# Second MLP layer of a fused attention block: two of seven products on a second level in six of eight units, with one row operation and one weight fold moved

## The chip, the cores and the metric

The kernel runs on one core of one Trainium2 chip. A core has five engines with queues of their own: TensorE (PE in the profile; its weight loads are the row PEld), VectorE (DVE), ScalarE (ACT), GpSimd (POOL) and SyncE (SP, which here issues DMAs). [...] The metric is the time of one execution on the device in microseconds (us), and the median over runs is compared.

## The reference

Two layers follow one another on an image `x` of 2 x 512 x 32 x 32 values (2 images, 512 channels, 1024 positions), all in float32.

```python
# layer 0: deformable attention with a bias from a small network per pair of positions, then an MLP
xn = bn(x); q = gconv1x1(xn); offsets = tanh(...)*4; kv = grid_sample(xn); k, v = gconv1x1(kv)
bias = relu(relu(pos @ w1) @ w2) @ w3            # for 1024 x 64 pairs, 8 heads, 2 images
x = x + out_w @ softmax(q k^T * scale + bias) v + out_b
xn2 = bn(x)
h1 = gelu(mlp_w1 @ xn2 + mlp_b1)                 # 512 -> 2048 channels
x = x + mlp_w2 @ h1 + mlp_b2                     # 2048 -> 512 channels
# layer 1: full attention over 1024 positions
q, k, v = x Wq^T + bq, x Wk^T + bk, x Wv^T + bv
x = x + (softmax(q k^T / sqrt(512)) v) Wp^T + bp
```

The change is in the MLP of layer 0, and touches two small preparations of layer 1 that run beside it.

## The kernel before

**Three stages.** The bias network takes about the first three quarters of the time (line 695 and its surroundings). Then, from about 1900 us on, come the output projection, the MLP and the attention of layer 1. The MLP lies between 1935 and 2307 us of the profiled span.

**Products.** All large products of the later stages are split once into two by two blocks and done with seven products of blocks instead of eight (the scheme of Strassen in Winograd's form). `PARTS` names, for each product 1 to 7, which of seven weight blocks meets which of seven moving blocks; blocks 4 to 6, and a rewritten block 3 or 1, are sums of the four original ones. `fold` makes the sums of weights, `spread` those of the moving side (four operations on VectorE: lines 125 and 128). A product of blocks is 256 x 256 weights times 256 x 512 values; `multiply` runs it with four matmuls of 512 columns into a pair of PSUM banks and then calls an eviction from `took`. Each float32 matmul is two instructions (passes) in the trace, so a product is 8 passes.

**A second level.** `twice` runs a pair of such products once more split, each into seven products of 128 x 128 weights and 256 columns. One step does one of the seven for both products of the pair: two matmuls of 256 columns, four passes (line 160). Steps share two half banks: steps 1, 6, 7 and 4 accumulate one after the other in one, steps 5 and 3 in another, step 2 has its own. So each result must be taken out before the next step may add to the same half bank. ScalarE (lines 166, 170, 172, 176) and VectorE (`plus`, line 137) take them out.

**The MLP's units.** Eight units (`units`): image b (0, 1) times a quarter p (0 to 3) of the 2048 hidden channels; unit i = 4 b + p. A unit runs `layer1` (512 -> 512 hidden channels, six products in three pairs with `twice`, one plain, then GELU by line 1101, result in the tile `hm`, then `spread` of `hm`) and `layer2` (512 hidden -> 512 channels, seven plain products, line 1082). Of `layer2`'s products four are kept over the units of an image in `acc` (`own`; ScalarE copies in the first unit of an image, line 1157, VectorE adds in the others), three are added into the image `xs` at once (`give`). `finish(b)` combines `acc` and adds the bias `mlp_b2` at the end of an image.

**Weights.** `load_first` and `load_inner` bring the next unit's first-layer weights (tiles `w1x` and `w1t` in turn, inner sums `w1e`), the sums made by accumulating DMAs that POOL issues (line 984, called gathers here). `load_second` loads `w2t` on SP when the unit before has read its last, and POOL folds it with four operations (line 119), behind the last gather in its queue. The point between two units, where `layer2` of one ends and `layer1` of the next begins, is called the seam here.

**Work beside it.** In each unit one row operation (line 1223) multiplies a row block `wr` of layer 1's weights with a bias row `br` and sums it into `ub`; `wr` has the buffer tag "ss" and is loaded by SP (line 1211). `load_g` brings `gg`, a product of layer 1's weights made earlier, with four loads on SP, and POOL folds it. `blocks(0)` makes sums of the finished image 0 with four VectorE operations (lines 971 to 974).

**What sets the order.** The order on each engine is fixed when the kernel is built: a scheduler places instructions by priority in program order, and `tc.issue_after(...)` holds an instruction behind a named one. Pools with a number of buffers decide which tile waits for which. `mq` hands out four PSUM tiles of two banks in turn.

Of the kernel before, what the change touches and what calls it, by code (L numbers as in the profile page):

```python
# [8 lines left out]
F32 = mybir.dt.float32  # L9
# [48 lines left out]
def conv_seq_kernel(ctx: ExitStack, tc: tile.TileContext, x, xt, kst, pst, cst, vec, wsm, outw, w1, w2, wl, wlt, brow, out):  # L58
# [82 lines left out]
    def twice(pool, sets, weights, moving, dest, done, fills=(), sign=-1.0):  # L141
# [3 lines left out]
        for _, g, q in sorted(todo, key=lambda e: e[0]):  # L145
# [31 lines left out]
            elif q == 3:  # L177
                plus(d12, d12, bank)
                done(g)

    FIRST_W, FIRST_X = (1, 0, 2, 3, 4, 5, 6), (1, 4, 0, 6, 5, 2, 3)
    AT_W, AT_X = ((0, 0), (1, 0), (1, 1), (0, 1)), ((0, 0), (0, 1), (1, 0), (1, 1))
# [794 lines left out]
    with ExitStack() as top, tc.tile_pool(name="wp", bufs=1) as wp:  # L977
# [28 lines left out]
        def load_second(i):  # L1006
            if i >= len(units):
                return
            w = wp.tile([P, 7, 2, 256], F32, tag="w2t", name="w2t")
            nc.sync.dma_start(out=w[:, 0:4], in_=w2[:, units[i][1]])  # L1010
            fold(nc.gpsimd, [w[:, j] for j in range(7)])
            wts[units[i]].append(w)

# [137 lines left out]

        def layer2(b, p, w, hm):

# [6 lines left out]
            def give(o2, h, op):  # L1160
                x_ = xs[:, 2 * o2 : 2 * o2 + 2, b, h * 512 : (h + 1) * 512]
                return lambda ps: plus(x_, x_, ps, op)

            multiply(mq, (2, 1, 3, 5, 6, 7, 4), product(w, hm), {
                1: own(0), 5: own(1), 6: own(2), 7: own(3),
                2: give(0, 0, ALU.add), 3: give(0, 1, ALU.add), 4: give(1, 0, ALU.subtract),
            })

        def finish(b):
            p1, p5, p6, p7 = (acc[:, j] for j in range(4))  # L1170
            for o in range(NCH):
# [32 lines left out]
        for i, (b, p) in enumerate(units):  # L1204
# [7 lines left out]
            with tc.issue_after(copied[-1]) if i else nullcontext():  # L1212
                load_first(i + 1)
            wa, we, wb = wts.pop((b, p))
            hm = cp.tile([P, 7, 2, 512], F32, tag="big", name="hm")
            layer1(p, we, wa, xb, xe, hm, ((4, lambda: part(1)), (10, lambda: part(2))) if p == 0 else (), i == 0)
            if i == NU:
# [3 lines left out]

            with tc.issue_after(newest(mybir.EngineType.DVE)):
                nc.vector.scalar_tensor_tensor(
                    wr, wr, 1.0, br, ALU.mult, ALU.mult, accum_out=ub[:, j, k : k + 1]
                )
            if p == NU - 1 and b == 0:
                xb = normalise(1)
            layer2(b, p, wb, hm)
            load_second(i + 1)
            if i == NU:  # L1230
                with tc.issue_after(newest(mybir.EngineType.SP)):
                    gg = f_pool.tile([P, 7, 2, 256], F32, tag="vp", name="gg")
                    load_g(gg, 0)
            if i == NU + 2:
                xbl = blocks(0)
# [368 lines left out]
```

## Time and profile before

| | us |
|---|---|
| median of 3 runs (2612.23 to 2612.84) | 2612.61 |
| the profiled execution | 2612.25 |
| its span | 2610.5 |
| MLP in the span, 1935.3 to 2307.2 | 371.9 |
| TensorE busy in it | 369.7 |
| VectorE busy in it | 255.6 |
| ScalarE busy in it | 120.8 |
| POOL busy in it | 117.9 |

The granted TensorE clock is 1.00 throughout the MLP, and the 16 DMA engines are busy for 0.66 of it. The busy times come from the view of windows. A line of the timeline has start, duration, engine, source line, operation, output<-input, shape and count, and in brackets how long the engine stood idle before and what released it. Consecutive like operations of an engine are merged into one line, so a duration can cover several. Matmuls overlap one another, and a matmul line's duration reaches past the start of the next one: the rate is read from starts.

### The profile page before, as it was taken

The numbers are of one execution on the slowest core, as the hardware profiler recorded it, in microseconds if no ns is written. First come the engines' busy times: TensorE is split into PE (matmuls) and PEld (weight loads), VectorE is DVE, ScalarE is ACT, GpSimd is POOL, SyncE is SP. The second block draws the span as 40 slices with busy tenths as digits, with TensorE's granted clock in tenths as the row PEclk, the third lists the DMA queues.
The fourth block names the chain that finished last, engine by engine and source line by source line (L and its number), as shares of the span: only waits on it lengthen the run. The fifth ranks groups of instructions, "written<-read, shape, count | busy, mean of one in ns | idle before, by whom it ended". The sixth has DMA issues, their size and how long they took to land.

```text
span 2610.5 us, 49004 instructions
## 1 busy us (share of the span) xinstructions
PE 2597.5 (100%) x19660; PEld 1009.8 (39%) x19660; DVE 2303.7 (88%) x1459; ACT 1754.3 (67%) x2362; POOL 980.6 (38%) x1122
## 2 busy tenths in 40 slices
PE   9999999999999999999999999999999999999999
PEld 3332333333233233223333333332355655646656
DVE  6999999999999999999999999999776587666656
ACT  5887888888888888888788777777733242314041
POOL 1344444444444444444454444333322334200100
PEclk9999999999999999999999999999999999999999
DMA  5889999999998999899999899888777768400202
GB/s 187 173 192 197 194 194 195 195 189 191 200 191 189 188 204 203 175 191 202 191 197 192 186 193 193 176 174 186 153 200 171 147 148 167 91 16 1 73 1 56
DMA packets 177634, 428.27 MB, mean 164 GB/s; under 512 B 30048, under 2 KB 78320, under 8 KB 174720
## 3 DMA queue, kind: packets, MB, share of 16 engines
q0 software_dynamic: 107392, 273.09, 58.4%
q1 hardware_dynamic: 69584, 151.75, 17.5%
q8 instruction: 155, 2.54, 0.4%
q14 instruction: 71, 0.58, 0.1%
q10 hardware_dynamic: 432, 0.31, 0.0%
HBM read 82.16 MB, written 6.55 MB: 34 GB/s over the span
## 4 chain that ended last, share of the span: by engine, by line
PE 96%; DVE 3%; ACT 1%; issue 0%; DMA 0%; DVEq 0%; ACTq 0%
PE ps L695 67%; PE sw L1082 7%; PE sw L1253 7%; PE sw L160 7%; PE sw L1029 2%; PE sw L1351 2%; PE psg L597 1%; PE sim L828 1%; DVE hm L137 1%; PE psx L1329 1%; PE sim L809 0%; PE pt L845 0%; PE pkv L534 0%; PE pb L880 0%; PE psq L333 0%
## 5 line engine op out<-in xcount | busy, mean ns | idle before, releaser
L695 PE MATMUL ps<-h,cw 128*32 128x512 f32 x16384 | 1772.0, 592 | 1.8 <-ACT rx L708 1.0
L678 DVE CUSTOM_DVE_ANT_1 h<-ta,tb 128x4096 f32<-128x4096 f32 (+1 forms) x257 | 1131.3, 4402 | 28.9 <-PE ps L695 24.0
L695 PEld LDWEIGHTS ps<-h,cw 128*32 128x32 f32 x16384 | 527.7, 110 | 1214.0 <-issue 1160.4
L708 ACT ACTIVATE rx<-ps,sc 128x1024 f32<-128x1024 f32 x512 | 568.6, 1111 | 138.4 <-PE ps L695 115.5
L737 POOL DMA_DIRECT2D u<-u x394 | 406.9, 1514 | 2.5 <-issue 2.2
L710 ACT ACTIVATE ub<-ps,sc 128x1024 f32<-128x1024 f32 x256 | 308.4, 1205 | 90.6 <-PE ps L695 90.5
L720 POOL DMA_DIRECT2D uo<-ub x127 | 111.4, 877 | 600.1 <-DVE ub L718 570.0
L718 DVE SCALAR_TENSOR_TENSOR ub<-rx,sc,ub 128x1024 f32<-128x1024 f32 x256 | 327.3, 1278 | 3.1 <-ACT ub L710 3.1
L1082 PE MATMUL sw<-hm,w2t 128*128 128x512 f32 x448 | 194.0, 592 | 0.2 <-DVE hm L125 0.2
L710 ACT ACTIVATE uo<-ps,sc 128x1024 f32<-128x1024 f32 x128 | 154.3, 1205 | 43.9 <-PE ps L695 40.7
L718 DVE SCALAR_TENSOR_TENSOR uo<-rx,sc,uo 128x1024 f32<-128x1024 f32 x128 | 163.7, 1279 | 7.6 <-ACT uo L710 7.0
L737 POOL DMA_DIRECT2D u<-uc x124 | 124.8, 1280 | 17.6 <-DMA u<-uc 15.3
L1082 PEld LDWEIGHTS sw<-hm,w2t 128*128 128x128 f32 x448 | 84.9, 190 | 104.0 <-issue 97.9
L720 POOL DMA_DIRECT2D uc<-ub x64 | 55.4, 866 | 179.9 <-DVE ub L718 147.9
L137 DVE TENSOR_TENSOR hm<-hm,sw 128x512 f32<-128x512 f32 x79 | 57.6, 732 | 73.0 <-PE sw L160 50.6
L720 POOL DMA_DIRECT2D u<-ub x62 | 53.1, 856 | 178.8 <-DVE ub L718 178.8
L737 POOL DMA_DIRECT2D uc<-uc x63 | 107.6, 1708 | 0.0
L737 POOL DMA_DIRECT2D uc<-uo x63 | 102.8, 1632 | 10.6 <-DMA uc<-uo 10.3
L1417 POOL DMA_DIRECT2D xs<-rs x6 | 7.2, 1200 | 259.6 <-DVE rs L137 259.6
L737 POOL DMA_DIRECT2D u<-uo x62 | 84.8, 1368 | 21.6 <-DMA u<-uo 18.4
L658 ACT ACTIVATE ta<-fb,vs 128x512 f32<-128x512 f32 (+1 forms) x65 | 89.1, 1374 | 5.6 <-DMA fb<-fdr 5.6
L710 ACT ACTIVATE uc<-ps,sc 128x1024 f32<-128x1024 f32 x64 | 77.0, 1203 | 21.2 <-PE ps L695 19.3
(306 smaller groups left out, 2648.2 us busy)
## 6 DMA issues: line engine op xcount, KB each, us to landing
uo<-ub POOLq DMA_DIRECT2D x127, 512.0 KB, 5.4
fb<-fdr SPq DMA_DIRECT2D x64, 512.0 KB, 5.7
uc<-ub POOLq DMA_DIRECT2D x64, 512.0 KB, 6.0
u<-ub POOLq DMA_DIRECT2D x62, 512.0 KB, 6.3
uc<-uc POOLq DMA_DIRECT2D x63, 256.0 KB, 8.3
uc<-uo SPq DMA_DIRECT2D x63, 256.0 KB, 3.2
uc<-uo POOLq DMA_DIRECT2D x63, 256.0 KB, 5.7
u<-u POOLq DMA_DIRECT2D x62, 256.0 KB, 6.9
```

The costliest lines, as they stand in the source:

```text
L137: nc.vector.tensor_tensor(out, a, b_, op)
L160: nc.tensor.matmul(bank[:, e, :], w, x, start=(q in (1, 2, 5) and e == k == 0), stop=True, skip_group_check=True,)
L658: nc.scalar.activation(ta.rearrange("p j x -> p x j")[:, :, j0:j1], fb[:, 0, :, j0:j1], AF.Identity, bias=col("cb1"), scale=col("w1x"),)
L678: nc.vector._custom_dve(TENSOR_ADD_SAT, out=h1[:, y : y + step].rearrange("p y t x -> p (y t x)"), in0=a.unsqueeze(1).to_broadcast([P, ste ...
L695: nc.tensor.matmul(ps[32 * q : 32 * q + 32, h, :], cw2[:, 32 * z : 32 * z + 32], h1[:, 16 * h : 16 * h + 16, q, :], start=True, stop=True,)
L708: nc.scalar.activation(o, ps, AF.Relu, bias=sc[:, 4 + z : 5 + z])
L710: nc.scalar.activation(o, ps, AF.Relu, bias=sc[:, 4 + z : 5 + z], scale=sc[:, z : z + 1])
L718: nc.vector.scalar_tensor_tensor(r[1], r[0], sc[:, z : z + 1], r[1], ALU.mult, ALU.add)
L720: nc.gpsimd.dma_start(out=sums[s][1], in_=sums[s][3], accum_op=ALU.add)
L737: nc.gpsimd.dma_start(out=out, in_=in_, accum_op=ALU.add)
L1082: nc.tensor.matmul(ps[:, m, :], w[:, a, k, m * P : (m + 1) * P], x[:, b_, k, :], start=(k == 0), stop=(k == 1),)
L1253: nc.tensor.matmul(ps[:, m, :], w[:, a, k, c + m * P : c + (m + 1) * P], x[b_][:, k, :], start=(k == 0), stop=(k == nk - 1),)
```

## The change

In units 0, 1, 2, 5, 6 and 7 `layer2` runs products 7 and 6 on the second level. They form one pair: steps 2 and 1 come after four plain products (2, 1, 3, 5), then product 4, then steps 6, 5, 7, 3, 4. Units 3 and 4 keep seven plain products in the old order. The pair's moving side needs three inner sums from `spread(xi)`, four VectorE operations of 128 x 512 values; two go into a new eighth block of `hm`, one into `hme`, a tile with the tag "ss" that `wr` also uses. Its weights need three inner sums in the new tile `w2e` and one rewritten block, four POOL operations behind each fold of `w2t`. `acc` blocks 2 and 3 swap the products that they keep.

The row operation moves from between `layer1` and `layer2` into `layer1`, at place 15.5 among its steps (after step 2 of the third pair, before step 4 of the second). `load_g` of `gg` moves from the end of unit 4 to ahead of `layer2` of unit 5.

```diff
@@ -178,6 +178,7 @@
                 plus(d12, d12, bank)
                 done(g)
 
+    TWO = slice(3, 6, 2)
     FIRST_W, FIRST_X = (1, 0, 2, 3, 4, 5, 6), (1, 4, 0, 6, 5, 2, 3)
     AT_W, AT_X = ((0, 0), (1, 0), (1, 1), (0, 1)), ((0, 0), (0, 1), (1, 0), (1, 1))
 
@@ -1009,7 +1010,11 @@
             w = wp.tile([P, 7, 2, 256], F32, tag="w2t", name="w2t")
             nc.sync.dma_start(out=w[:, 0:4], in_=w2[:, units[i][1]])
             fold(nc.gpsimd, [w[:, j] for j in range(7)])
-            wts[units[i]].append(w)
+            we = None
+            if i not in (NU - 1, NU):
+                we = wp.tile([P, 2, 3, P], F32, name="w2e")
+                fold(nc.gpsimd, inner_w(w, we, TWO, slice(0, 2)))
+            wts[units[i]] += [w, we]
 
         for i, (b, h) in enumerate(halves):
             for o in range(NCH):
@@ -1149,7 +1154,7 @@
             twice(mq, ((1, 6), (4, 7), (5, 3)), weights, moving, dest, done, (*plain, *others))
             spread([hm[:, j] for j in range(7)])
 
-        def layer2(b, p, w, hm):
+        def layer2(b, p, w, hm, we=None):
 
             def own(j):
                 a = acc[:, j]
@@ -1161,13 +1166,66 @@
                 x_ = xs[:, 2 * o2 : 2 * o2 + 2, b, h * 512 : (h + 1) * 512]
                 return lambda ps: plus(x_, x_, ps, op)
 
-            multiply(mq, (2, 1, 3, 5, 6, 7, 4), product(w, hm), {
-                1: own(0), 5: own(1), 6: own(2), 7: own(3),
+            took = {
+                1: own(0), 5: own(1), 7: own(2), 6: own(3),
                 2: give(0, 0, ALU.add), 3: give(0, 1, ALU.add), 4: give(1, 0, ALU.subtract),
-            })
+            }
+            plain = product(w, hm)
+            if we is None:
+                multiply(mq, (2, 1, 3, 5, 6, 7, 4), plain, took)
+                return
+
+            far = hm[:, 7].rearrange("p a (b n) -> p a b n", n=256)
+            last = f_pool.tile([P, 2, 256], F32, tag="ss", name="hme")
+            xi = [hm[:, 1:6:4, k, 256 * n : 256 * n + 256] for k, n in AT_X] + [far[:, 0], far[:, 1], last]
+            wi = inner_w(w, we, TWO, slice(0, 2))
+            d11, d12, d21, d22 = (acc[:, 2:4, m, 256 * h : 256 * h + 256] for m in range(2) for h in range(2))
+
+            def into(d, bank, op=ALU.add, new=False):
+                if new and p == 0:
+                    nc.scalar.activation(d, bank, AF.Copy, scale=1.0 if op == ALU.add else -1.0)
+                else:
+                    plus(d, d, bank, op)
+
+            def inner(bank, q):
+                u, t = PARTS[q]
+                with tc.issue_after(newest(mybir.EngineType.PE)):
+                    for e in range(2):
+                        nc.tensor.matmul(
+                            bank[:, e, :], wi[u][:, e], xi[t][:, e], start=(q in (1, 2, 5) and e == 0), stop=True,
+                            skip_group_check=True,
+                        )
+
+            def whole(q):
+                with tc.issue_after(newest(mybir.EngineType.PE)):
+                    multiply(mq, (q,), plain, took)
+
+            for q in (2, 1, 3):
+                whole(q)
+            with tc.issue_after(newest(mybir.EngineType.DVE)):
+                spread(xi)
+            whole(5)
+            side, main = (mq.tile([P, 2, 512], F32, tag="ps2", name="sw") for _ in range(2))
+            two, five = (side[:, h].rearrange("p (e n) -> p e n", e=2) for h in range(2))
+            one = main[:, 0].rearrange("p (e n) -> p e n", e=2)
+            inner(two, 2)
+            into(d11, two, new=True)
+            inner(one, 1)
+            into(d11, one)
+            whole(4)
+            inner(one, 6)
+            into(d12, one, new=True)
+            inner(five, 5)
+            into(d22, five, ALU.subtract, new=True)
+            inner(one, 7)
+            into(d22, one, ALU.subtract)
+            inner(five, 3)
+            into(d12, five)
+            inner(one, 4)
+            into(d21, one, ALU.subtract, new=True)
 
         def finish(b):
-            p1, p5, p6, p7 = (acc[:, j] for j in range(4))
+            p1, p5, p7, p6 = (acc[:, j] for j in range(4))
             for o in range(NCH):
                 nc.scalar.activation(xs[:, o, b, :], xs[:, o, b, :], AF.Identity, bias=col("mb2", o))
             v = [xs[:, o2 : o2 + 2, b, n : n + 512] for o2 in (0, 2) for n in (0, 512)]
@@ -1211,26 +1269,30 @@
             nc.sync.dma_start(out=wr, in_=wlt[:, i])
             with tc.issue_after(copied[-1]) if i else nullcontext():
                 load_first(i + 1)
-            wa, we, wb = wts.pop((b, p))
-            hm = cp.tile([P, 7, 2, 512], F32, tag="big", name="hm")
-            layer1(p, we, wa, xb, xe, hm, ((4, lambda: part(1)), (10, lambda: part(2))) if p == 0 else (), i == 0)
+            wa, we, wb, wbe = wts.pop((b, p))
+            hm = cp.tile([P, 8, 2, 512], F32, tag="big", name="hm")
+
+            def row():
+                with tc.issue_after(newest(mybir.EngineType.DVE)):
+                    nc.vector.scalar_tensor_tensor(
+                        wr, wr, 1.0, br, ALU.mult, ALU.mult, accum_out=ub[:, j, k : k + 1]
+                    )
+
+            others = ((4, lambda: part(1)), (10, lambda: part(2))) if p == 0 else ()
+            layer1(p, we, wa, xb, xe, hm, (*others, (15.5, row)), i == 0)
             if i == NU:
                 with tc.issue_after(newest(mybir.EngineType.DVE)):
                     finish(0)
             load_inner(i + 1)
 
-            with tc.issue_after(newest(mybir.EngineType.DVE)):
-                nc.vector.scalar_tensor_tensor(
-                    wr, wr, 1.0, br, ALU.mult, ALU.mult, accum_out=ub[:, j, k : k + 1]
-                )
             if p == NU - 1 and b == 0:
                 xb = normalise(1)
-            layer2(b, p, wb, hm)
-            load_second(i + 1)
-            if i == NU:
+            if i == NU + 1:
                 with tc.issue_after(newest(mybir.EngineType.SP)):
                     gg = f_pool.tile([P, 7, 2, 256], F32, tag="vp", name="gg")
                     load_g(gg, 0)
+            layer2(b, p, wb, hm, wbe)
+            load_second(i + 1)
             if i == NU + 2:
                 xbl = blocks(0)
             if p == NU - 1 and b == 0:
```

## The prediction

> **What bounds the kernel now.** I read the page first (busy shares, then the chain that ended last), then the timeline over one unit of the MLP, then the two units with extra VectorE work. Lines: page; timeline of units 2 and 3; timeline of VectorE and TensorE in unit 6.
>
> ```profile
> span 2610.5 us, 49004 instructions
> PE 2597.5 (100%) x19660; PEld 1009.8 (39%) x19660; DVE 2303.7 (88%) x1459; ACT 1754.3 (67%) x2362; POOL 980.6 (38%) x1122
> ...
> PE 96%; DVE 3%; ACT 1%; issue 0%; DMA 0%; DVEq 0%; ACTq 0%
> ```
>
> ```profile
> 2052.05 24.20 PE L1082 MATMUL sw<-hm,w2t 128*128 128x512 f32 x56
> ...
> 2076.09 1.89 PE L160 MATMUL sw<-xb,w1t 128*128 128x256 f32 x8
> ...
> 2076.28 1.22 DVE L137 TENSOR_TENSOR xs<-xs,sw 128x1024 f32<-128x1024 f32 x1 [2.21 <-PE sw L1082]
> ...
> 2078.08 0.69 DVE L137 TENSOR_TENSOR hm<-hm,sw 128x512 f32<-128x512 f32 x1 [0.58 <-PE sw L160]
> 2078.82 0.73 PEld L160 LDWEIGHTS sw<-xe,w1e 128*128 128x128 f32 x4 [0.26 <-DVE hm L137]
> ...
> 2083.24 1.89 PE L160 MATMUL sw<-xe,w1e 128*128 128x256 f32 x8
> ...
> 2084.97 1.03 PE L160 MATMUL sw<-xb,w1e 128*128 128x256 f32 x4
> ...
> 2086.83 3.00 DVE L137 TENSOR_TENSOR hm<-hm 128x1024 f32<-128x1024 f32 x1
> ...
> 2087.15 6.26 POOL L119 TENSOR_TENSOR w2t<-w2t 128x512 f32<-128x512 f32 x4
> ...
> 2091.08 1.13 PE L160 MATMUL sw<-xe,w1e 128*128 128x256 f32 x4 [0.76 <-DVE hm L137]
> ```
>
> ```profile
> 2246.14 1.22 DVE L125 TENSOR_TENSOR hm<-hm 128x1024 f32<-128x1024 f32 x1
> ...
> 2252.42 1.22 DVE L137 TENSOR_TENSOR xs<-xs,sw 128x1024 f32<-128x1024 f32 x1
> ```
>
> ```profile
> 2247.50 13.97 PE L1082 MATMUL sw<-hm,w2t 128*128 128x512 f32 x32 [0.24 <-DVE hm L125]
> ```
>
> TensorE is the bound, and in the MLP it almost never stops. Layer 2 of unit 2 runs from 2052.05 to 2076.09: 24.04 us for 56 passes, 0.4293 us each, no gap. A step of four 256-column passes takes 0.865 us (2083.24 to 2084.97 is two). The rest is small waits. One is the handoff: a step ends at 2077.83, VectorE adds it at 2078.08 for 0.69 us, and the next weight load for that bank starts at 2078.82; with the first load uncovered (about 0.1 us), 1.09 us pass from a step's end until its bank is in use again, against 0.865 us of other work. Another is VectorE being slow while POOL folds w2t: 3.00 us instead of 1.22, and TensorE stands.
>
> **The change, part by part.** The sum is made against the profiled execution, 2612.25 us (span 2610.5 and 1.75 around it); the median of the runs is 0.36 higher.
>
> *TensorE's work.* In units 0, 1, 2, 5, 6, 7 two products (16 passes, 16 x 0.4293 = 6.87 us) become seven steps (7 x 0.865 = 6.05). That is -0.82 a unit, -4.9 in all, before any wait. This is already under 0.2% of the time (5.2 us), which is about what a measurement of this kernel can tell from no change.
>
> *The new handoffs.* Step 2 and step 1 stand ahead of product 4 (3.43 us), and steps 6, 5, 7, 3, 4 follow it back to back on two half banks. VectorE must give product 4 (1.21 us, starting 0.20 after its end, like 2076.28) before it takes step 6. Counting from the end of product 4: give 0.20, step 6's add from 1.33 (the next add starts 1.13 after a 1.21 us one) to 2.02; step 7 effectively at 2.17 instead of 1.73, +0.44. Step 7 ends at 3.03, its add runs 3.28 to 3.97, step 4 starts at 4.12 instead of 3.90, +0.22. So +0.66 in units 1, 2 and 5: +2.0. In unit 0 ScalarE takes four of these results in 0.59 us (row L166), so step 7 comes 0.10 late, steps 3 and 4 some 0.25: +0.35. Ahead of that nothing is late: with the row gone, VectorE ends the new sums (4 x 0.68, row of 128x512 sums) 15.6 us into layer 2 and step 1's add at 18.1, and its bank is wanted at 18.7.
>
> *Unit 7.* The instruction order puts two of finish(1)'s adds (1.23 us) between the evictions: one before step 1's add, which now ends at 19.06 instead of before 18.69 (+0.32 at step 6), one before step 7's (step 4 waits 0.88), and step 7 waits 0.22: +1.4.
>
> *Unit 6.* Here VectorE also builds blocks(0) (four 1.22 us operations) and is full from 2235.27; product 5 already waits (2247.50). In the new order product 4's give stands before step 1's add. Counting from 2236.80: product 3's give ends at 16.2 (15.6 + 1.2 less the 0.6 of the row), so product 4 starts at 16.40 instead of 15.93 (+0.47) and ends at 19.83. Then the give, and only then step 1's add, 21.45 to 22.14; step 6, wanting that bank, starts at 22.29: +2.46. Handoffs again 2 x 0.22. In all +3.4. Attention's fold moves to layer 2 of unit 5, at POOL ahead of that unit's last gathers, so unit 6's gathers and w2t's fold come some 2 us later (before: fold at 2226.59, 11.6 after the seam), onto two 1.22 us sums and blocks(0)'s first; slowed by about 0.5 each as at a fold (1.87 and 1.69 were seen in unit 5), less 0.49 of idle time: +1.0 (bounds 0 and 3).
>
> *The four new POOL operations a unit.* Half of w2t's (1.27 undisturbed), so 2.6 us. In unit 0 they delay w1t's gathers, which today start the moment the fold ends (1946.56), and by this unit 1's fold, from 10.8 us after the seam to about 12, past the 1.22 us sum that it stretches today to 2.72 (1993.93): TensorE's 0.75 there goes, -0.75 (bounds -0.75 and +0.3). In units 1, 2, 5 and 7 they reach the last sums of layer 1, where the first GELU has 1.06 us to spare: together +0.65 (bounds 0 and 3). [...]
>
> *The row.* 0.68 us leaves layer 2, where it delayed an add that TensorE did not wait for: nothing by itself. In layer 1 it falls into VectorE's idle time (2.09 us before 2093.11), even if stretched by a fold: 0, bound +0.5 a unit in units 2 and 3. Its load now follows w2t's at the seam, as hme shares its buffer. w2t lands 8.3 us after issue, a row 4.9 (medians), one after the other 13.2; the row is due 13.3 after the seam, and only from 15.3 is the next add late. So 0. The 256 KB at the seam can also shift the gathers, and so the fold in units 2 and 3, whose waits today are 0.46 and 1.03: bounds -1.5 and +1.
>
> *Attention's fold.* In layer 2 of unit 5 POOL reaches it behind the third w1e gather, some 16 us in, when VectorE has only adds out of PSUM left: 0 there. Its four loads (0.75 + 1.30 + 1.70 + 0.83 us of issue) leave the seam and stand on SP behind unit 6's w1e copies and ahead of unit 7's w1 load, which so lands some 4.6 us later, at 2207.7 instead of 2203.1 (2193.50 + 9.6), and POOL's first gather of it is at 2213.37: 0. gg itself is first read after unit 7.
>
> *Sum.* -4.9 + 2.0 + 0.35 + 1.4 + 3.4 + 1.0 - 0.75 + 0.65 = +3.1: 2615.4 us.
>
> **Rivals.**
> A, *handoffs hidden*: VectorE frees the half banks in time and unit 6's order does not reach TensorE. For it: the windows show VectorE busy 18.86 of 27 us there (2049 to 2076), and twice() already runs such steps with 0.24 us lost a unit. Against: there no 1.21 us give precedes them. Time: 2612.25 - 4.9 - 0.75 + 0.65 = 2607.2.
> B, *the row late*, slower: its load lands after 15.3 us, VectorE stands in front of it, and step 3 of layer 1's second set finds its bank full. A landing at 16.5 costs 1.2 in each of seven units, 8.4, and with the 3.1 gives 2623.8; it decides (slower by over 5.2) from a landing at 15.6 on. Against: the landing medians above; for it: w2t took up to 9.8, and unit 4 loads br as well.
> C, *VectorE's backlog as in unit 6, elsewhere too*: the folds delay layer 2's first sums, so step 1's add misses its 0.5 us of slack in units 1, 2, 5, 7 by 1 us each and unit 6 takes its upper bound: +3.1 + 4 + 2 = 2621.
>
> **How the numbers follow.** Forecast 0.72, A 0.10, B 0.06, C 0.12. The forecast's own bounds (new waits between half and one and a half times 8.1, folds at their ends) are 2610 to 2619.5; A lies below and B and C above. The range 2609.3 to 2620 leaves 0.2 out. Faster by over 0.2% is part of A: 0.07. Slower is B, C and the forecast's upper edge: 0.19. Within: 0.74.
>
> **What would show it.** Per unit, layer 2 should last 23.9 us in 1, 2, 5 (24.04 before), 23.6 in 0, 24.6 in 7, 27 or 28 in 6. TensorE's waits at the new line should name VectorE's acc, longest (some 2.5) in unit 6. In layer 1 of unit 1 the 2.72 us sum should be back at 1.22. The row should start without waiting for a DMA. I am wrong if layer 2 lasts 23.2 us throughout, or if layer 1 grows by over 0.5 us a unit.

## The result, and the profile after

The changed kernel takes 2618.93 us (median of 15 runs, 2617.28 to 2620.42), the kernel before 2612.75 us in the same comparison (15 runs, 2611.74 to 2613.98): a ratio of 1.0022, 95% interval 1.0015 to 1.0030. All 15 runs lie above the slowest run of the kernel before, so it is slower, by about 0.2%. The prediction was 2615.4 us in a range of 2609.3 to 2620.0. The profiled execution of the changed kernel took 2617.67 us, against 2612.25 before.

The page of the changed kernel (span, busy shares, and the chain that ended last by engine):

```profile
span 2615.7 us, 49247 instructions
PE 2597.6 (99%) x19732; PEld 1023.5 (39%) x19732; DVE 2334.5 (89%) x1511; ACT 1754.4 (67%) x2364; POOL 1005.2 (38%) x1146
...
PE 83%; DVE 6%; issue 4%; DMA 3%; POOL 2%; ACT 1%; DVEq 0%; POOLq 0%; ACTq 0%
```

TensorE's busy time is the same as before (2597.5), although by the prediction's working it has 4.9 us less to compute. It covers matmuls that overlap and whose ends are modelled, so it can't carry the reading. The span has grown by 5.2 us, and TensorE's share of the chain has fallen from 96% to 83%.

Where it grew is read by laying out the start of the first matmul of each layer in each unit. All values are us in the two profiled executions.

| unit | layer 1 before | after | layer 2 before | after | unit's change |
|---|---|---|---|---|---|
| 0 | 22.79 | 24.43 | 24.06 | 23.72 | +1.30 |
| 1 | 22.56 | 21.80 | 24.03 | 23.91 | -0.88 |
| 2 | 22.27 | 21.82 | 24.03 | 23.91 | -0.57 |
| 3 (plain) | 22.85 | 21.82 | 24.03 | 24.03 | -1.03 |
| 4 (plain) | 22.13 | 22.58 | 24.03 | 24.03 | +0.45 |
| 5 | 21.82 | 21.82 | 24.03 | 26.07 | +2.04 |
| 6 | 21.82 | 21.82 | 24.51 | 28.32 | +3.81 |
| 7 | 21.82 | 21.82 | 24.03 | 23.56 | -0.47 |

The sum is +4.65. The other 0.55 of the span arose ahead of the MLP, in a stage that the change does not touch (the first matmul of unit 0 starts between 1936.3 and 1937.6 us in the traces of all the kernels here). In unit 0 the 0.86 us of one matmul that the scheduler of the kernel before draws from layer 2 into layer 1 is counted in layer 2. In unit 7 the changed kernel runs six passes of the next stage inside layer 2 (2.58 us); they are taken out of the 26.14 us.

Four places carry it. The first two are in the timeline of unit 6, VectorE and then TensorE:

```profile
2257.72 0.68 DVE L128 SCALAR_TENSOR_TENSOR hme<-hm 128x512 f32<-128x512 f32 x1
2258.32 0.68 DVE L137 TENSOR_TENSOR acc<-acc,sw 128x512 f32<-128x512 f32 x1
2258.92 1.21 DVE L137 TENSOR_TENSOR xs<-xs,sw 128x1024 f32<-128x1024 f32 x1
2260.05 0.68 DVE L137 TENSOR_TENSOR acc<-acc,sw 128x512 f32<-128x512 f32 x1
```

```profile
2254.92 3.70 PE L1087 MATMUL sw<-hm,w2t 128*128 128x512 f32 x8 [0.18 <-DVE xs L137]
2260.88 2.59 PE L1194 MATMUL sw<-hm,w2e 128*128 128x256 f32 x8 [2.25 <-DVE acc L137]
2263.26 1.91 PE L1194 MATMUL sw<-hm,w2t 128*128 128x256 f32 x4
2264.97 1.29 PE L1194 MATMUL sw<-hm,w2e 128*128 128x256 f32 x4
```

Product 4 ends at about 2258.4 (2254.92 and eight passes of 0.43). Step 6 can't start until step 1's result is out of the half bank, and VectorE takes it only at 2260.05, after product 4's give (2258.92): 2.4 us of standing. Then the passes themselves are slow: the step from 2263.26 takes 1.71 until the next starts, not 0.94. The windows say why: the third column from the end is the granted clock, 0.66 between 2260.9 and 2265.9.

```profile
2260.90:2265.90 5.00, 5.00 (x16) 4.05 (x16) 2.06 (x3) 0.00 (x0) 0.00 (x0) 0.66 0.00 0
```

The third place is unit 5, VectorE, POOL and TensorE of the same timeline:

```profile
2203.70 2.75 DVE L125 TENSOR_TENSOR hm<-hm 128x512 f32<-128x512 f32 x1
2206.49 1.64 DVE L128 SCALAR_TENSOR_TENSOR hm<-hm 128x512 f32<-128x512 f32 x1
2208.05 0.68 DVE L125 TENSOR_TENSOR hm<-hm 128x512 f32<-128x512 f32 x1
...
2203.17 1.43 POOL L985 DMA_DIRECT2D w1e<-w1e  x1 [5.40 <-DMA w1e<-w1x]
2204.03 3.55 POOL L119 TENSOR_TENSOR gg<-gg 128x512 f32<-128x512 f32 x2
...
2211.99 1.97 PE L1194 MATMUL sw<-hm,w2e 128*128 128x256 f32 x8 [2.19 <-DVE acc L137]
```

The third gather of `w1e` came at 2203.17, 12.4 us into layer 2. So two operations of attention's fold met the first two new sums, which took 2.75 and 1.64 us instead of 0.68 each; everything behind them on VectorE is late, and step 6 stands for 2.35 us.

The fourth is unit 0, TensorE, first before, then after:

```profile
1956.34 1.13 PE L160 MATMUL sw<-xb,w1x 128*128 128x256 f32 x4 [0.21 <-ACT hm L170]
1957.30 1.02 PE L1082 MATMUL sw<-hm,w2t 128*128 128x512 f32 x2
1958.16 1.12 PE L160 MATMUL sw<-xe,w1x 128*128 128x256 f32 x4
```

```profile
1956.88 1.13 PE L160 MATMUL sw<-xb,w1x 128*128 128x256 f32 x4 [0.21 <-ACT hm L170]
1958.70 1.13 PE L160 MATMUL sw<-xe,w1x 128*128 128x256 f32 x4 [0.69 <-ACT hm L172]
1959.66 1.03 PE L160 MATMUL sw<-xb,w1e 128*128 128x256 f32 x4
1961.31 1.98 PE L1087 MATMUL sw<-hm,w2t 128*128 128x512 f32 x4 [0.62 <-ACT hm L1106]
```

Before, a matmul of layer 2 (1957.30) fills a wait of layer 1. After, the same wait stands open, and another 0.62 us opens ahead of layer 2.

Against all this the changed kernel gains in layer 1 of units 1 to 3: the first 1.22 us sum of layer 1, stretched by `w2t`'s fold before (2.72 us in unit 1; experiment 8 shows the line), keeps its 1.2 us now. VectorE in unit 1 after:

```profile
1995.76 1.23 DVE L137 TENSOR_TENSOR hm<-hm 128x1024 f32<-128x1024 f32 x1
```

The sum begins 10.7 us after the seam. The fold began 11.3, 12.9 and 11.7 us after it in units 1, 2 and 3, where it had begun at 10.8, 10.5 and 11.1. A few tenths decide, as the last section shows. Unit 4, where the sum begins at 11.1, lost its 0.45 us the opposite way: the fold began at 10.8 instead of 11.9 and stretched the sum from 1.23 to 2.35 us.

### The profile page after: what moved, and what is told of

Read it like the earlier page. It is cut to its first block, busy times and chain, and to the rows that moved or that the text cites. A ratio compares the mean times of both kernels' runs of the same rounds, so it can differ in the third digit from the quotient of the medians.

```text
span 2615.7 us, 49247 instructions
## 1 busy us (share of the span) xinstructions
PE 2597.6 (99%) x19732; PEld 1023.5 (39%) x19732; DVE 2334.5 (89%) x1511; ACT 1754.4 (67%) x2364; POOL 1005.2 (38%) x1146
## 4 chain that ended last, share of the span: by engine, by line
PE 83%; DVE 6%; issue 4%; DMA 3%; POOL 2%; ACT 1%; DVEq 0%; POOLq 0%; ACTq 0%
PE ps L696 56%; PE sw L1315 7%; PE sw L160 6%; PE sw L1087 4%; DMA u<-uc 2%; PE sw L1034 2%; PE sw L1413 2%; POOL u L738 1%; PE sw L1194 1%; DVE hm L137 1%; PE psg L598 1%; DVE h L679 1%; PE sim L829 1%; DVE ub L719 1%; PE psx L1391 1%
## 5 line engine op out<-in xcount | busy, mean ns | idle before, releaser
L679 DVE CUSTOM_DVE_ANT_1 h<-ta,tb 128x4096 f32<-128x4096 f32 (+1 forms) x257 | 1130.9, 4401 | 28.6 <-PE ps L696 23.9
L719 DVE SCALAR_TENSOR_TENSOR ub<-rx,sc,ub 128x1024 f32<-128x1024 f32 x256 | 326.9, 1277 | 3.1 <-ACT ub L711 3.1
L1087 PE MATMUL sw<-hm,w2t 128*128 128x512 f32 x352 | 153.8, 593 | 1.0 <-ACT hm L1106 0.6
L738 POOL DMA_DIRECT2D uc<-uo x63 | 101.9, 1617 | 12.1 <-DMA uc<-uo 11.7
L1087 PEld LDWEIGHTS sw<-hm,w2t 128*128 128x128 f32 x352 | 66.6, 190 | 80.3 <-issue 72.4
```

The costliest lines, as they stand in the source:

```text
L679: nc.vector._custom_dve(TENSOR_ADD_SAT, out=h1[:, y : y + step].rearrange("p y t x -> p (y t x)"), in0=a.unsqueeze(1).to_broadcast([P, ste ...
L719: nc.vector.scalar_tensor_tensor(r[1], r[0], sc[:, z : z + 1], r[1], ALU.mult, ALU.add)
L738: nc.gpsimd.dma_start(out=out, in_=in_, accum_op=ALU.add)
L1087: nc.tensor.matmul(ps[:, m, :], w[:, a, k, m * P : (m + 1) * P], x[:, b_, k, :], start=(k == 0), stop=(k == 1),)
```

## The experiments

Each was compared with the kernel before on the same chip. The intervals of the ratios reach some 0.0009 to each side, 2.3 us. A smaller difference of medians can't be told from none, so each verdict goes by the unit in question in the profiled execution.

**1. Attention's fold back in unit 4.** Theory 1: the loss in unit 5 is this fold falling on the new sums. The rival is the new order of steps as such.

```diff
-            if i == NU + 1:
-                with tc.issue_after(newest(mybir.EngineType.SP)): ... load_g(gg, 0)
             layer2(b, p, wb, hm, wbe)
             load_second(i + 1)
+            if i == NU:
+                with tc.issue_after(newest(mybir.EngineType.SP)): ... load_g(gg, 0)
```

> The changed kernel with attention's fold 0 (its four loads and four POOL operations) put back to the end of unit 4, behind that unit's layer 2. Theory: the 2.35 us wait in layer 2 of unit 5 comes from this fold meeting the new 128x512 sums (2.75 and 1.64 us instead of 0.68), so layer 2 of unit 5 falls from 26.07 to about 23.9 us, as in units 1 and 2, and the four sums are back at 0.7 us; profiled time some 2615.5 (after: 2617.67). Rival: the wait belongs to the order of the new steps in that unit, whatever POOL does: layer 2 of unit 5 stays at 26 us. Unit 6, which neither theory ties to the fold alone, stays near 28.3, or loses up to 1 us if its gathers come 2 us earlier again.

Measured: 2617.86 us (11 runs), ratio 1.0020 (1.0011 to 1.0029). Layer 2 of unit 5 lasts 25.49 us, not 23.9: the number is the rival's. But the reason is not. The timeline of VectorE and POOL in that run:

```profile
2191.71 6.06 DVE L137 TENSOR_TENSOR hm<-hm 128x1024 f32<-128x1024 f32 x3
...
2190.99 7.91 POOL L119 TENSOR_TENSOR gg<-gg 128x512 f32<-128x512 f32 x4
```

Put back, the fold falls on three of the 1.22 us sums at the start of layer 2 (6.06 us for the three), and VectorE carries the delay of some 2.4 us through to step 1's add. In the kernel before the fold stood in the same place and cost nothing, because layer 2 had no new sums and VectorE had the time. So neither place is safe once layer 2 gives VectorE 2.7 us of new sums. Theory 1 became: the fold costs wherever it meets sums in layer 2 of unit 5.

**2. Unit 6 plain.**

```diff
-            if i not in (NU - 1, NU):
+            if i not in (NU - 1, NU, NU + 2):
```

> The changed kernel with the old seven plain products in layer 2 of unit 6. Theory: the give of product 4 ahead of step 1's add, on a VectorE that also builds blocks(0), makes the wait, and the 256-column passes at 0.43 us behind it follow from the wait; both go: layer 2 of unit 6 from 28.3 to about 24.5 us as before, granted clock 1.0 there, profiled time some 2613.9 (after: 2617.67). Rival: later folds and gathers of the changed kernel (the fold of attention in unit 5) keep unit 6 late whatever its order: layer 2 of unit 6 stays above 26 us, and the time above 2615.5.

Measured: 2613.77 us, ratio 1.0005 (0.9997 to 1.0014). Layer 2 of unit 6 is 24.51 us, as the theory said: 3.81 us come from putting the second level there. The profiled execution was the longest of its 11 runs (2616.90), with 27.69 us in layer 2 of unit 5, where the fold again met the new sums (2.91 and 1.64 us) and the granted clock fell as well (0.55 from 2212.4 to 2216.2 us).

**3. Unit 0 plain.** `0` was added to the same list.

> The changed kernel with the old seven plain products, whose order the scheduler may choose, in layer 2 of unit 0. Theory: the 1.64 us that layer 1 of unit 0 gained come from the fixed order of its products, which forbids the scheduler to start with product 1 and to draw its first matmul into a wait: layer 1 of unit 0 back at 22.8 us with 0.86 of layer 2 within it, layer 2 24.06 with that, the unit at 46.9 instead of 48.15, profiled time some 2616.4 (after: 2617.67). Rival: layer 1 of unit 0 is late for another reason (the row, the loads at the seam): the unit stays at 48 us or goes to 48.5, since the 0.34 us that layer 2 gained is lost too.

Measured: 2615.45 us, ratio 1.0012 (1.0003 to 1.0021). Unit 0 is back at 46.85 us, to the hundredth. In this execution the third gather of unit 5 came 15.7 us into layer 2, so the fold began only after the last new sum:

```profile
2203.09 0.68 DVE L125 TENSOR_TENSOR hm<-hm 128x512 f32<-128x512 f32 x1
2203.80 0.69 DVE L128 SCALAR_TENSOR_TENSOR hm<-hm 128x512 f32<-128x512 f32 x1
...
2205.85 1.43 POOL L985 DMA_DIRECT2D w1e<-w1e  x1 [8.68 <-DMA w1e<-w1x]
2206.70 3.22 POOL L119 TENSOR_TENSOR gg<-gg 128x512 f32<-128x512 f32 x2
```

Layer 2 of unit 5 then lasts 23.91 us, as in units 1 and 2. The order of steps is the same in both executions; only the fold's time differs. That rules out the rival of experiment 1.

**4. The three together** (second level in units 1, 2, 5, 7; fold back in unit 4).

> The three of this call together: second level in units 1, 2, 5 and 7 alone, attention's fold 0 back at the end of unit 4, unit 0 free to choose. Theory: the three losses are independent and add up: 2617.67 - 2.2 - 3.8 - 1.3 = 2610.4 us profiled, 0.07% below the kernel before. Rival: the work taken from one place waits at the next (POOL's folds onto the 1.22 us sums of another unit), and the time stays at or above 2612.3.

Measured: 2613.58 us, ratio 1.0004 (0.9995 to 1.0013); profiled 2614.58. Units 0 and 6 are as before (46.85 in all, and 24.51 in layer 2), but layer 2 of unit 5 is 26.88: the fold put back costs there, as in experiment 1. The gains of the two plain units add up; the one that rested on theory 1 in its first form doesn't come.

**5. The row alone**, on the kernel before.

```diff
+            def row():
+                with tc.issue_after(newest(mybir.EngineType.DVE)):
+                    nc.vector.scalar_tensor_tensor(wr, wr, 1.0, br, ...)
-            layer1(p, we, wa, xb, xe, hm, (...), i == 0)
+            layer1(p, we, wa, xb, xe, hm, (*others, (15.5, row)), i == 0)
 ...
-            with tc.issue_after(newest(mybir.EngineType.DVE)):
-                nc.vector.scalar_tensor_tensor(wr, wr, 1.0, br, ...)
```

> The kernel before with the row alone moved (into layer 1, behind slot 15.5, in each unit); layer 2 stays seven plain products and attention's fold 0 stays in unit 4. Theory: the row costs nothing where it stands; what moves is the place of w2t's fold, since w2t's load now stands ahead of the row's on SP. So layer 2 stays at 24.03 us, and layer 1 of a unit is 21.8 us where the first 1.22 us sum keeps that length and up to 1.1 us more where the fold meets it; the time within 1.5 us of 2612.3. Rival: the row itself, stretched to some 1.8 us by the fold, makes the next step wait 0.5 us or more in most units: layer 1 above 22.3 us in units 1 to 7 and the time at 2615 or above.

Measured: 2613.03 us against 2613.09, ratio 1.0001 (0.9992 to 1.0009). Layer 1 of units 1 to 7 is 22.32, 22.32, 21.82, 23.09, 21.91, 22.15 and 21.82, together 155.43 us against 155.27 before. Single units move by up to 1 us with the place of `w2t`'s fold (in unit 3 it began 11.2 instead of 11.1 us after the seam and the sum took 1.23 instead of 3.00 us, in unit 4 11.3 instead of 11.9 and 2.93 instead of 1.23); the total does not.

**6. Unit 0's order alone**, on the kernel before.

```diff
-            multiply(mq, (2, 1, 3, 5, 6, 7, 4), product(w, hm), {...})
+            for q in (2, 1, 3, 5, 6, 7, 4):
+                with tc.issue_after(newest(mybir.EngineType.PE)) if (b, p) == units[0] else nullcontext():
+                    multiply(mq, (q,), product(w, hm), took)
```

> The kernel before with one edit: the seven plain products of layer 2 in unit 0 are each fixed behind TensorE's newest instruction, in the written order 2, 1, 3, 5, 6, 7, 4, as the changed kernel does. Theory: this order alone makes unit 0's loss, since product 2 needs a GELU that ends later than product 1's: layer 1 of unit 0 from 22.8 (and 0.86 of layer 2 within it) to 24.4 us, layer 2 24.0, the unit from 46.85 to some 48.45 us, profiled time 2613.9. Rival: the scheduler's draw of one matmul into a wait was worth nothing, or the second level itself made the loss: the unit stays within 0.4 us of 46.85 and the time within 0.5 of 2612.3.

Measured: unit 0 takes 24.43 + 24.14 = 48.57 us, 1.72 more than 46.85, with the two waits of the changed kernel at the same places:

```profile
1958.09 1.13 PE L160 MATMUL sw<-xe,w1x 128*128 128x256 f32 x4 [0.69 <-ACT hm L172]
1959.05 1.02 PE L160 MATMUL sw<-xb,w1e 128*128 128x256 f32 x4
1960.69 2.84 PE L1082 MATMUL sw<-hm,w2t 128*128 128x512 f32 x6 [0.62 <-ACT hm L1101]
```

The median is 2614.00 against 2613.09, ratio 1.0004 (0.9995 to 1.0013), profiled 2614.61. The unit's loss is the pinned order's, not the second level's.

**7. Product 4's give last**, on the changed kernel.

```diff
+            kept, held = took[4], []
+            took[4] = held.append
             whole(4)
 ...
             into(d21, one, ALU.subtract, new=True)
+            with tc.issue_after(newest(mybir.EngineType.DVE)):
+                kept(held[0])
```

> The changed kernel with product 4's add into xs (1.21 us of VectorE) put behind the adds of all seven steps of the second level. Theory: this add is what makes step 7 late by 0.22 us in units 1, 2 and 5 beyond the plain handoff, and what stands before step 1's add in unit 6. So layer 2 goes from 23.91 to about 23.7 us in units 1 and 2; in unit 6 the wait at step 6 shrinks from 2.41 to some 1.3 us and layer 2 from 28.3 to 26.9, or to some 25.3 if the slower passes behind the wait come from its length. Unit 5 depends on where attention's fold falls. Profiled time 2613.5 to 2615.5. Rival: the handoff of a bank itself (1.09 us against 0.865 of other work) is all of it: 23.91 and 28.3 stay, time 2617.7.

Measured: 2615.45 us, ratio 1.0010 (1.0001 to 1.0019). Layer 2 of units 1 and 2 lasts 23.64 us, as the theory said. TensorE in unit 1, first the changed kernel, then this one:

```profile
2025.73 1.89 PE L1194 MATMUL sw<-hm,w2e 128*128 128x256 f32 x8
2027.89 1.10 PE L1194 MATMUL sw<-hm,w2t 128*128 128x256 f32 x4 [0.28 <-DVE acc L137]
2028.83 1.03 PE L1194 MATMUL sw<-hm,w2e 128*128 128x256 f32 x4
```

```profile
2025.49 1.89 PE L1194 MATMUL sw<-hm,w2e 128*128 128x256 f32 x8
2027.39 1.10 PE L1194 MATMUL sw<-hm,w2t 128*128 128x256 f32 x4
```

Step 7 starts 2.16 us after step 6 in the one and 1.90 in the other. In unit 6 the wait at step 6 is nearly gone (a start 0.24 us late instead of 2.4), but layer 2 still lasts 28.16 us: this time `w2t`'s and `w2e`'s folds came late there (POOL began the first 6.64 us ahead of layer 2 and not 10.04), stretched blocks(0)'s first operation to 2.24 us and two sums to 1.75, and product 5 stood for 2.4 us instead. Its eight passes then took 5.20 us where the changed kernel needs 3.51 (granted clock 0.68).

```profile
2248.23 5.37 PE L1087 MATMUL sw<-hm,w2t 128*128 128x512 f32 x8 [2.27 <-DVE hm L125]
```

So taking the give away doesn't save unit 6: the wait stands at whichever product VectorE reaches too late. What the give alone costs there this run doesn't show, as the late folds came with it. In unit 7 layer 2 takes 24.00 us with the give last, not 23.56, and experiments 9 and 10 leave it in its place there.

**8. `w2t`'s fold held behind the first sum of layer 1**, on the kernel before: a tiny POOL addition, which reads what that sum wrote, stands ahead of the fold.

```diff
+            def folds(src):
+                if src is None:
+                    fold(nc.gpsimd, [w[:, j] for j in range(7)])
+                    return
+                nc.gpsimd.tensor_tensor(tick, src[:, 0, 0:2], src[:, 0, 0:2], ALU.add)
+                with tc.issue_after(newest(mybir.EngineType.Pool)):
+                    fold(nc.gpsimd, [w[:, j] for j in range(7)])
-            fold(nc.gpsimd, [w[:, j] for j in range(7)])
+            pending.append(folds)
 ...
+            if i:
+                others += ((12.5, lambda: pending.pop()(hm[:, 1])),)
```

> The kernel before with w2t's fold on POOL made to wait for the first 1.22 us sum of layer 1 (a tiny POOL addition that reads that sum's result stands ahead of it), in units 1 to 7; nothing of the change is in it. Theory: what layer 1 of units 1 to 4 spends above 21.82 us in the kernel before (0.74, 0.45, 1.03 and 0.31) is this sum stretched by the fold, and the changed kernel gained 2.2 us in units 1 to 3 only because its loads shift the fold: with the fold behind the sum all of units 1 to 7 have 21.8 us, and the time falls by 2.5 to 2609.7 us. Rival: the fold then meets the two sums of the second set of steps, whose GELU layer 2 waits for: layer 1 grows by 0.3 to 1 us in each of seven units and the time is 2614 or above.

Measured: 2611.24 us (11 runs, 2610.61 to 2611.79) against 2613.09, ratio 0.9994 (0.9985 to 1.0003). Unit 1 before (VectorE, POOL, TensorE), then with the fold held:

```profile
1993.93 2.72 DVE L137 TENSOR_TENSOR hm<-hm 128x1024 f32<-128x1024 f32 x1
...
1993.96 6.27 POOL L119 TENSOR_TENSOR w2t<-w2t 128x512 f32<-128x512 f32 x4
...
1997.89 1.13 PE L160 MATMUL sw<-xe,w1e 128*128 128x256 f32 x4 [0.48 <-DVE hm L137]
```

```profile
1994.32 1.23 DVE L137 TENSOR_TENSOR hm<-hm 128x1024 f32<-128x1024 f32 x1
...
1995.63 0.19 POOL L1017 TENSOR_TENSOR tick<-hm 128x2 f32<-128x2 f32 x1 [1.17 <-DVE hm L137]
1995.78 5.07 POOL L119 TENSOR_TENSOR w2t<-w2t 128x512 f32<-128x512 f32 x4
...
1996.78 1.89 PE L160 MATMUL sw<-xe,w1e 128*128 128x256 f32 x8
```

Layer 1 of units 1 to 3 is 21.82 us each: 2.22 us gained, which is what the changed kernel has there too (-2.24). It had them without any such hold, by where its folds happened to fall. Units 4 and 5 did not follow (22.14 and 22.05). In unit 4 the sum had its 1.23 us in the kernel before too, so the 0.31 us that the theory put on the fold there are not the fold's. In unit 5 attention's fold now ran ahead of `w2t`'s and stretched two later sums to 2.25 and 1.68 us (1.87 and 1.69 before). The units together gain 1.9 us and not 2.5; the span gains 1.5, as the stage ahead of the MLP took 0.4 longer. The ratio's interval holds 1, so it is the units that show the gain, not the medians.

Beside a fold these sums of SBUF tiles got longer: 2.72 against 1.23 us for the same sum here, 2.75 against 0.68 in unit 5 of the changed kernel. Adds out of PSUM beside `w2t`'s fold kept their 0.68 us (unit 1, at 1996.56 in the kernel before and at 1996.90 in the changed one). What makes the two kinds differ no run here shows.

**9 and 10. Everything mended.** The second level in units 0, 1, 2, 5 and 7 with the order of unit 0's plain products free, the give last in units 1, 2 and 5, the folds of `w2t` and `w2e` held behind the first sum, and attention's fold held behind the last new sum of unit 5 (the edits of 2, 7 and 8, and):

```diff
             with tc.issue_after(newest(mybir.EngineType.DVE)):
                 spread(xi)
+            if summed is not None:
+                nc.gpsimd.tensor_tensor(tick, last[:, 0, 0:2], last[:, 0, 0:2], ALU.add)
+                with tc.issue_after(newest(mybir.EngineType.Pool)):
+                    fold(nc.gpsimd, summed)
```

> The changed kernel with every loss found so far mended: second level in units 0, 1, 2, 5 and 7 (unit 6 plain); unit 0's four plain products free in order; product 4's add into xs last in units 1, 2 and 5; w2t's and w2e's folds held until the first 1.22 us sum of layer 1 is done, attention's fold 0 held until the last new sum of unit 5 is done (each by a tiny POOL addition that reads the sum). Theory: against the 2612.25 us profiled before, unit 0 gains 0.34, layer 1 of units 1 to 5 some 2.0 (as the held fold gave alone), layer 2 of units 1, 2 and 5 0.39 each (23.64 instead of 24.03), unit 7 0.44: 4.0 in all, 2608.3 us. Rival: w2e's folds, now later, run onto the first sums of layer 2, and step 1's add comes late in units 1, 2, 5 and 7 by 0.5 to 1 us: layer 2 above 24.2 there, and 2610.5 us or more.

The second of the two has unit 0 plain as well:

> As e9_all_mended, but with seven plain products in unit 0 too (second level in units 1, 2, 5 and 7). Theory: unit 0 as in the kernel before, 46.85 us, so 0.34 us slower than e9_all_mended, some 2608.6 us profiled. Rival: with w2e's four POOL operations gone from unit 0, the gathers of unit 1 come earlier and its fold too, but the fold is held behind the sum: no change beyond that 0.34; were the hold worth nothing, layer 1 of unit 1 would be 22.4 us again, as in the runs with unit 0 plain.

Measured: 2609.97 us (11 runs, 2609.01 to 2610.48), ratio 0.9987 (0.9978 to 0.9996), and 2609.67 us (2608.89 to 2610.68), ratio 0.9986 (0.9977 to 0.9995), both against 2613.18. Both are faster than the kernel before, by 3.2 and 3.5 us. In the second, layer 2 lasts 23.64 us in units 1, 2 and 5, and layer 1 21.82 in units 1 to 3; neither rival showed. The profiled executions took 2610.14 and 2610.10 us, though, where 2608.3 and 2608.6 were expected: the stage ahead of the MLP took 0.7 us longer, layer 1 of unit 4 stays at 22.31 us, and layer 2 of unit 6, plain, lasts 24.94 and 25.04 us instead of 24.51, as its product 5 waits 0.67 and 0.71 us instead of 0.24.

In the first of the two, the second level in unit 0 shortens that unit by 0.41 us, and unit 2 gives 0.35 of it back (22.03 in layer 1 and 23.78 in layer 2), so no gain from it is seen. In units 1, 2, 5 and 7 the second level is worth about 1.6 us by the units: 3 x 0.39, and 0.4 in unit 7. The medians fit that (3.5 us here, 1.9 in experiment 8, each against the kernel before), but their intervals overlap.

**11. Attention's fold held, on the changed kernel alone.**

> The changed kernel with attention's fold 0 held on POOL until the last new sum of layer 2 in unit 5 is done. Theory: the 2.35 us wait of unit 5 is this fold meeting the new sums, which depends on when the third gather of w1e comes (12.4 us into layer 2 in the changed kernel's profile, 15.7 and 16.3 in two others, in which layer 2 lasted 23.9 and 23.6); held, it can't meet them: layer 2 of unit 5 at 23.91 us, profiled time 2615.5 if unit 6 stays at 28.3, and single runs spread less than the 3.1 us of the changed kernel. Rival: the sums are slowed by something else in unit 5: it stays at 25.5 to 27.7 us, and so does the spread.

Measured: 2616.60 us (11 runs, 2615.47 to 2618.58), ratio 1.0014 (1.0005 to 1.0023). VectorE and TensorE in unit 5:

```profile
2204.17 0.68 DVE L125 TENSOR_TENSOR hm<-hm 128x512 f32<-128x512 f32 x1
...
2212.28 1.10 PE L1196 MATMUL sw<-hm,w2t 128*128 128x256 f32 x4 [0.28 <-DVE acc L137]
```

Layer 2 of unit 5 lasts 23.90 us, and the only wait is that of units 1 and 2. But the gather came 17.1 us in, so the hold had nothing to hold back in this execution (nor in the profiled ones of experiments 9 and 10, with 16.4 and 15.8). What settles unit 5 is the place of the fold: behind a gather at 12.4 and 12.6 us (the changed kernel, experiment 2) layer 2 lasts 26.07 and 27.69 us, behind one at 15.7, 16.3 and 17.1 (experiments 3, 7 and this one) 23.91, 23.64 and 23.90. The spread of single runs (3.1 us) is no smaller than the changed kernel's, so unit 5 is not all of it.

**12. blocks(0) out of unit 6**, on the changed kernel.

```diff
-            if i == NU + 2:
-                xbl = blocks(0)
+            if i == NU + 3:
+                with tc.issue_after(newest(mybir.EngineType.DVE)):
+                    xbl = blocks(0)
```

> The changed kernel with blocks(0), VectorE's four 1.22 us operations for attention, fixed behind the adds of unit 7's steps instead of running in layer 2 of unit 6. Theory: these 4.9 us are what unit 6 lacks: without them its VectorE order is that of units 1 and 2 and its layer 2 lasts 23.9 us instead of 28.3; the stage after unit 7, which needs their results, may start later by up to 4.9 us, so the time is between 2613.3 and 2618. Rival: the late gathers and folds in unit 6 keep it late without blocks(0) too: layer 2 of unit 6 above 25.5 us.

Measured: 2614.27 us (10 runs), ratio 1.0005 (0.9996 to 1.0015). Layer 2 of unit 6 falls from 28.32 to 24.42 us, even though the folds came late in this execution too (first sum of the second set 2.40 us). The long wait at step 6 is down to a short one:

```profile
2256.86 1.97 PE L1194 MATMUL sw<-hm,w2e 128*128 128x256 f32 x8 [0.44 <-DVE acc L137]
```

From the start of unit 7's layer 2 to the end it takes 328.6 us instead of 326.9: blocks(0) costs 1.7 us there. So the 4.9 us of VectorE work for attention are what unit 6 lacks, as the prediction said. The rest (24.42, not 23.91) goes with the late folds, by the timeline.

## Why the prediction was right, and where it was not

The median lies 3.5 us above the predicted 2615.4 and inside the range, and the ratio's interval (1.0015 to 1.0030) holds the 0.2% bound, so the prediction's cases "within 0.2%" and "slower by over 0.2%" can't be told apart. Laid out by units, with TensorE's -0.82 in each of the six and the 0.65 for the POOL operations spread over its four, the prediction's terms against the measured changes are:

| unit | 0 | 1 | 2 | 3 | 4 | 5 | 6 | 7 | sum |
|---|---|---|---|---|---|---|---|---|---|
| predicted | -0.47 | -0.75 | 0.0 | 0 | 0 | 0.0 | +3.58 | +0.74 | +3.1 |
| measured | +1.30 | -0.88 | -0.57 | -1.03 | +0.45 | +2.04 | +3.81 | -0.47 | +4.65 |

The total is near because misses of both signs stand in it, and that is luck: units 0 and 5, whose steps failed, cost 3.8 us more than was worked out, and units 2, 3 and 7 gave back 2.8. The rest up to the median is 0.55 us from the stage ahead of the MLP, 0.2 around the span, and the median's 1.3 over the profiled execution.

- *TensorE's work* and *the new handoffs* held. Layer 2 of units 1 and 2 lasts 23.91 us where 23.9 was predicted, so rival A (handoffs hidden) is out. With the give last (experiment 7) it is 0.27 less; the working had put 0.22 of the 0.66 on the give.
- *Unit 6* held in its mechanism, as experiments 2 and 12 show. Counted from the start of layer 2, step 1's add, worked out at 21.45 us, came at 21.41, and step 6, worked out at 22.29, at 22.24: the wait of 2.4 us is as predicted. Experiment 1 shows the term by itself. There the granted clock stays at 1.00, and layer 2 lasts 27.06 us against 24.51 - 0.82 + 3.4 = 27.1. The changed kernel needs 28.32, for a reason that the prediction has no term for, the granted clock (0.66): from step 6 to the unit's end 6.07 us pass, against 4.82 in experiment 1, so 1.25 us are slow passes.

```profile
2260.32 1.97 PE L1194 MATMUL sw<-hm,w2e 128*128 128x256 f32 x8 [2.26 <-DVE acc L137]
...
2265.14 1.89 PE L160 MATMUL sw<-xb,w1t 128*128 128x256 f32 x8
```

  (experiment 1; the second line is the unit's end.) The +1.0 for a later fold did not come in the changed kernel's profile, whose fold began 11.8 us after the seam, as before. It came in experiments 3 and 11: there the fold began 13.7 and 14.4 us after the seam, product 5 stood 1.45 and 1.52 us instead of 0.24, and layer 2 lasts 28.38 and 28.34 us, with the granted clock at 1.00 in experiment 3 (2259.5 to 2264.5 us). So it is luck that the unit's +3.81 is so near to +3.58: the slow passes stood in for the late fold.
- *Attention's fold: 0* failed; unit 5 lost 2.04 us. The step said that POOL reaches the fold "behind the third w1e gather, some 16 us in, when VectorE has only adds out of PSUM left". The gather came 12.4 us in. In four other executions with the fold at this place in POOL's order (experiments 2, 3, 7 and 12) it came at 12.6, 15.7, 16.3 and 17.0, and layer 2 lasted 27.69, 23.91, 23.64 and 23.91. The step took the landing of one execution for a fixed time and had no price for an earlier one. Rival C described such a backlog, but put it on the folds of the weights, 1 us in each of units 1, 2, 5 and 7.
- *Unit 0* failed by a term that is missing. Layer 2 saved 0.34 us where 0.47 was worked out, but layer 1 grew by 1.64: the scheduler had filled a wait of layer 1 with a matmul of layer 2, and the order fixed in `whole` excludes that. Experiment 6 gives that order's price alone, 1.72 us.
- *Unit 7: +1.4* failed in size. Waits cost some 0.35 us there (-0.47 + 0.82): TensorE fills them with six passes of the next stage. That this is why was read from the timeline only.
- *The four new POOL operations*: unit 1's -0.75 came (-0.76), and in the way that was worked out: without unit 0's four operations (experiments 3 and 4) layer 1 of unit 1 takes 22.38 and 22.48 us, not 21.80. No run shows the +0.65, which was the author's estimate: the later sums of layer 1 are stretched (1.65 us in unit 1, 1.82 in unit 5), but layer 1 stays at 21.8 us in units 1, 2, 5 and 7. In units 2 and 3 the fold's move gave -1.48 us, at the edge of the bounds (-1.5 to +1) of a term that was entered as 0, and in unit 4, which had no term, +0.45. Experiment 8 shows the mechanism by itself; what moved the fold in units 2 to 4, the row's load or the new POOL operations, stays open (the row alone, in experiment 5, has it begin at 10.5, 11.2 and 11.3).
- *The row: 0* held. It started without waiting for a DMA, and experiment 5 finds no change in the sum of the units. Rival B is out.

## What to carry to other kernels

Where two engines slow one another, as VectorE and POOL did here (2.72 against 1.23 us for one sum), a term of the sum is not "this operation costs 0.7 us" but "whom does it meet, and does a transfer's landing decide that": then it needs two prices and a chance, or a data dependence that makes the meeting impossible. A two-element operation of 0.2 us was enough for that, and by the units it was worth about as much as the second level (1.9 us, against some 1.6). And ahead of fixing an order by hand, look in the order before for work that the scheduler had drawn into a wait.

## What the runs showed of the hardware

TensorE's clock fell behind some waits inside the MLP and not behind others of the same length. At the same wait in unit 6 (2.25 us by the profile in the changed kernel, 2.26 in experiments 1 and 3) the granted clock of the next 5 us was 0.66 in the one and 1.00 in the two others:

```profile
2260.30:2265.30 5.00, 4.97 (x21) 3.81 (x22) 2.75 (x4) 0.00 (x0) 0.00 (x0) 1.00 0.00 0
```

(windows of experiment 1). A wait of 2.34 us in unit 5 of experiment 2 was followed by 0.55 over the next 3.8 us, one of 2.27 in unit 6 of experiment 7 by 0.68 over the next 5.3 us, one of 2.19 in unit 5 of the changed kernel by 1.00. The length of the wait alone doesn't decide it; no run here shows what does. From step 6 to the unit's end it took 6.07 us in the changed kernel's unit 6 and 6.28 in experiment 2's unit 5, against 4.82 in experiments 1 and 3, so the slow stretch cost 1.25 and some 1.45 us there.

Where `w2t`'s fold and the first sum of layer 1 met, which of the two was drawn out went with their starts. In the 14 traces here, the sum took 1.75 to 3.00 us wherever the fold began from 0.9 us ahead of it to 0.33 us behind it, most at 0.33 (3.00 us, unit 3 of the kernel before); wherever the fold began 0.46 us behind it or later, the sum took 1.23 us and the fold's first operation was the longer one (1.90 us at 0.46, 1.76 at 0.60 in unit 1 of the changed kernel, against 1.27 as the median of the fold's operations before). So 0.13 us of a start made 1.8 us of a sum.
